# First pair's neighbour scores spread by TensorE and masked from PSUM; the output weights' column sums moved behind the first attention

## The chip, the cores and the metric

The kernel runs on one core of a Trainium2 chip. A core has five engines with an instruction queue each: TensorE (PE; its weight loads are listed apart as PEld), VectorE (DVE), ScalarE (ACT), GpSimd (POOL) and SyncE (SP), which issues most of the DMAs; ScalarE issues some. Data lie in SBUF or, for TensorE's results, in PSUM (eight banks of 128 partitions by 512 f32). The metric is the device time of one execution in microseconds (us); lower is better.

## What is computed

128 graphs of 128 nodes with 512 features each go through a graph attention layer (8 heads of 64 units) and a hypergraph convolution, each with a residual and a layer norm. Cut to what matters here:

```python
# layer 0, per graph; A is the 0/1 adjacency
feats = X @ W[h]                                   # 8 heads of 64
e_self, e_neigh = feats . a_self, feats . a_neigh  # two scores per node and head
dense = leaky_relu(e_self[:, None] + e_neigh[None, :], 0.2) + NEG_BIG * (1 - A)
out = relu(softmax(dense) @ feats + b)
x = layernorm(x + out)
# layer 1; R = D^-1 H B^-1 H^T from the adjacency
h = layer_norm(relu(R @ (x @ W1^T) + b1), gamma, beta)
x = layernorm(x + (R @ (h @ W2^T) + b2) + x)
```

All of it is f32.

## The kernel before

**Tiling.** The graphs go in 64 pairs. A pair passes through five overlapping stages, T = 38.6 planned us apart: loads and masks; features and scores; softmax and attention; the hidden product; output and store. In the steady state TensorE runs without gaps, using Strassen's seven products for 2x2 blocks of the weights (`chain`, copied by line 329), which need sums of weight blocks: four of `w0` (`prepare_first_sums`, line 211), four of `w1` (`prepare_hidden`, line 234), and four of `w2` (`prepare_output_block_sums`).

**Order.** Every step is a small function with a due time. `steps` holds those of all pairs, `first` gives other times for single steps of the first pairs, `todo` holds what is done once (weights and their preparation). All are sorted by time and emitted in that order, which is then the order of each engine's queue, and of each DMA queue. An engine takes its instructions strictly in that order, so one that waits holds up all behind it. Only the order counts, not the planned times.

**The first pair (p = 0).** Its features are 32 plain products (line 510), copied into `ft` with the two scores as the first two columns of each head (line 520). To spread a neighbour's score over all partitions, `spread_rows` transposes the score columns into `rows` (line 529), writes them to DRAM by four DMAs (line 537, two on SP, two on ScalarE's queue), and `neighbours` reads them back to all 128 partitions, 512 KB for each graph, as `nb` (line 557). GpSimd then adds the mask `neg` in four quarters (`masked`, line 576; a quarter is one graph g and one half of the heads, q). ScalarE adds a node's own score and applies the leaky relu (`leaky`, line 592); for the last quarter of the first pair VectorE does so (lines 585 and 588). VectorE takes the negated maximum (`largest`, line 598), ScalarE the exponential (line 606). `e_transpose_first` turns the first pair's exponentials by TensorE (line 638), with the copies to `eT` shared by VectorE and ScalarE (line 639). `attend` multiplies by the features (line 662), `attended` divides (lines 676 and 677), GpSimd adds the bias (686), VectorE the residual and the moments (693 to 707), GpSimd takes the power for the inverse deviation (709), ScalarE normalises (725 to 734) into `y`. `propagate` multiplies `y` by R (line 757, `pz`), ScalarE evicts it to `zT` (769), GpSimd makes its block sums `zS` (780), and the hidden products follow (792).

**Second pair.** Its rows go out in one DMA (539), its scores come back in two (557), into the same buffer `nb`, of which there is one: the reading has to wait until the first pair's exponentials are transposed. It has its masks, leaky relu, maxima and exponentials while the first pair is in the hidden products; ScalarE's copies of `phX`, which TensorE waits for before it adds the next product to that bank, stand in the same ScalarE queue.

**Nodes and edges.** For R: `nodes` (345 to 354) and `edges` (406 to 413) count on VectorE, `scale_edges` (420) scales, `propagator` multiplies (429), `r_evict` (437) scales again with `dnb`, which has gone through DRAM. For the first two pairs `edges` reads a transposition in PSUM.

**The output weights.** gamma and the mean are folded into `w2`: `prepare_output` forms two column sums (gamma/DH and beta) with 16 small products, 32 records (261, `pv`), `prepare_output_sums` copies them (269), `prepare_output_spread` spreads them over the partitions as `gw` and `bw` (273), `prepare_output_bias` copies `bw` (278), and `prepare_output_blocks` scales and shifts the four blocks of `w2` on VectorE, four instructions each (285).

Of the kernel before, what the change touches and what calls it, by code (L numbers as in the profile page):

```python
# [8 lines left out]
F32 = mybir.dt.float32  # L9
AF = mybir.ActivationFunctionType  # L10
ALU = mybir.AluOpType
# [3 lines left out]
SLOPE = 0.2  # L15
# [5 lines left out]
def kernel(  # L21
# [45 lines left out]
    nc = tc.nc  # L67
    G, N, F = x.shape
    P = 128
    DH = w1t.shape[1]  # L70
    H = 8
# [17 lines left out]
    def bank(name):  # L89
        return psum.tile([P, HALF], F32, tag="bank", name=name)  # L90
# [433 lines left out]
    @step(1, 25.0)  # L524
    def spread_rows(p, s):


        rows = work.tile([P, B], F32, tag="rows", name=f"rows_{p}")
        nc.vector.transpose(
            rows.rearrange("p (c x) -> p c x", c=2),  # L530
            s["ft"][:, :, :, :2].rearrange("p g h c -> p c (g h)"),
        )
        shape = [B, NB, B] if p == 0 else [NB, B, B]
        rd = s["rd"] = dram.tile(shape, F32, tag="rd", name=f"rd_{p}")
        if p == 0:
            for b in range(NB):
                (nc.sync, nc.scalar)[b % 2].dma_start(rd[:, b, :], rows[b * B:(b + 1) * B])
        else:
            nc.sync.dma_start(rd.rearrange("b c j -> (b c) j"), rows)
# [6 lines left out]
    @step(1, 27.0)  # L546
    def neighbours(p, s):
        s["nb"] = work.tile([P, 2, H * N], F32, tag="nb", name=f"nb_{p}")
        for g in range(2):
            dst, src, hs = s["nb"][:, g, :], s["rd"], slice((2 + g) * H, (3 + g) * H)  # L550
            if p == 0:
                src = src[hs].rearrange("h b j -> (h b j)")
            else:
                dst = dst.rearrange("p (b x) -> p b x", b=NB)
                src = src[:, hs, :].rearrange("b h j -> b (h j)")
            queue = nc.scalar if p == 0 and g == 1 else nc.sync
            queue.dma_start(dst, src.partition_broadcast(P))
# [10 lines left out]
    def scores(p, s, g, hs):  # L568
        return blocked(p, s["nb"][:, g, :])[:, :, hs, :]
# [3 lines left out]
    def masked(p, s, g, q):  # L573
        t = scores(p, s, g, slice(q * HH, (q + 1) * HH))
        neg = s["neg"][:, g].rearrange("p (b j) -> p b j", b=NB)
        nc.gpsimd.tensor_tensor(  # L576
            t, t, neg[:, :, None, :].to_broadcast([P, NB, HH, B]), op=ALU.add
        )

    def leaky(p, s, g, q):  # L580
        if (p, g, q) == (0, 1, 1):

            hs = slice(HH, H)
            t = s["nb"][:, g, HH * N:].rearrange("p (h j) -> p h j", h=HH)
            nc.vector.tensor_tensor(
                t, t, s["ft"][:, g, hs, 0:1].to_broadcast([P, HH, N]), op=ALU.add
            )
            nc.vector.scalar_tensor_tensor(t, t, SLOPE, t, op0=ALU.mult, op1=ALU.max)
            return
        for h in range(q * HH, (q + 1) * HH):  # L590
            t = scores(p, s, g, h)
            nc.scalar.activation(t, t, AF.Prelu, bias=s["ft"][:, g, h, 0:1], alpha=SLOPE)  # L592
# [432 lines left out]
    for t, fn, *args in (  # L1025
# [28 lines left out]
        (98.1, prepare_output_bias, ()), (98.2, prepare_output_blocks, (slice(0, 1),)),  # L1054
        (99.75, prepare_output_blocks, (slice(1, 2),)),
# [17 lines left out]
        ("leaky", 0, 1, 1): 77.65,  # L1073
# [12 lines left out]
    for p, time, fn, *args in (  # L1086
# [84 lines left out]
```

## Time and profile before

The median of four runs is 2528.41 us (2528.16 to 2528.68). The profiled execution took 2528.16 us; its span, from the first to the last instruction, is 2526.4 us.

| | PE | DVE | ACT | POOL |
|---|---|---|---|---|
| busy, us of the span | 2498.9 | 1919.8 | 1539.6 | 1792.4 |
| share | 99% | 76% | 61% | 71% |

From the timeline of the first pair and of the start of the second, us from the span's start:

| | start | end |
|---|---|---|
| first pair's features (510), last copy (520) | 10.63 | 20.69 |
| scores broadcast from DRAM (557), issue to landing | 23.55 | 28.4 |
| first pair's masks on GpSimd (576) | 28.38 | 33.33 |
| column sums `pv` (261) | 29.46 | 36.53 |
| first pair's exponentials (606) | 33.31 | 38.08 |
| first pair's attention `pav` (662), with the last transposition between | 38.98 | 43.20 |
| first `pz` (757) | 50.70 | 54.40 |
| second pair's first maximum (598) | 56.28 | 56.97 |
| pace of a pair in the steady state (`pyX` at 239.31, 277.97, 316.64) | 38.67 | |

How to read it: an instruction group is given by its line in the source, engine, operation, output and inputs. A busy engine is not by itself the bound; the wait that ends last in a stage is. A f32 product of 128x128 by 128 shows as two records of TensorE, a transposition as one.

### The profile page before, as it was taken

How to read it: one execution, taken by the hardware profiler on the slowest of the kernel's cores; microseconds unless marked ns; L12 is line 12 of the kernel's file. 1: busy time of each engine (PE TensorE's matmuls, PEld its weight loads, DVE VectorE, ACT ScalarE, POOL GpSimd, SP SyncE). 2: the span in 40 equal slices, each digit the busy share in tenths (PEclk: the TensorE clock that was granted, in tenths of full speed). 3: DMA queues.
4: the chain of work that ended last, by engine and by line, in shares of the span. 5: the costliest groups of instructions: out<-in, count | busy, mean ns of one | idle time of the engine just before them, and what ended most of it. 6: DMA issues, size and time to landing. Idle time of an engine off the chain costs nothing.

```text
span 2526.4 us, 48492 instructions
## 1 busy us (share of the span) xinstructions
PE 2498.9 (99%) x16349; PEld 2269.8 (90%) x16349; DVE 1919.8 (76%) x4332; ACT 1539.6 (61%) x4481; POOL 1792.4 (71%) x2058
## 2 busy tenths in 40 slices
PE   7999999999999999999999999999999999999998
PEld 5899999999999999999999999999899999999997
DVE  7877777777777777777777777777777777777765
ACT  4565665755756656657557566566575665665753
POOL 5867777776777677767766776777677767777774
PEclk9999999999999999999999999999999999999999
DMA  6545445444444454454454444544544444445431
GB/s 184 135 135 142 137 132 152 132 129 147 132 135 142 137 143 137 128 151 134 125 152 133 136 139 139 144 136 125 152 131 130 145 137 140 137 131 151 134 110 51
DMA packets 420840, 343.76 MB, mean 136 GB/s; under 512 B 141272, under 2 KB 370160, under 8 KB 420592
## 3 DMA queue, kind: packets, MB, share of 16 engines
q1 hardware_dynamic: 417120, 336.19, 45.0%
q10 hardware_dynamic: 3472, 4.47, 0.6%
q8 instruction: 131, 2.15, 0.3%
q14 instruction: 117, 0.96, 0.1%
HBM read 238.83 MB, written 101.71 MB: 135 GB/s over the span
## 4 chain that ended last, share of the span: by engine, by line
PE 97%; DVE 1%; DMA 1%; issue 0%; POOL 0%; ACT 0%; SPq 0%; POOLq 0%; DVEq 0%; ACTq 0%
PE phX L792 18%; PE pyX L473 17%; PE phW L792 9%; PE pfX L473 9%; PE pav L662 9%; PE pyW L473 8%; PE pz L757 5%; PE phY L792 4%; PE pq L919 4%; PE pfW L473 4%; PE pyY L473 4%; PE pfY L473 2%; PE pd L429 1%; PE pf L510 1%; PE pm L887 1%
## 5 line engine op out<-in xcount | busy, mean ns | idle before, releaser
L329 ACT COPY py<-pyX 128x257 f32<-128x257 f32 x189 | 70.8, 375 | 539.3 <-PE pyX L473 523.3
L792 PEld LDWEIGHTS phX<-zS,w_sb 128*128 128x128 f32 x3072 | 363.1, 192 | 33.0 <-issue 31.6
L792 PE MATMUL phX<-zS,w_sb 128*128 128x128 f32 x3072 | 374.3, 275 | 2.4 <-POOL xS L455 1.3
L845 POOL TENSOR_TENSOR sq<-sq 128x512 f32<-128x512 f32 (+2 forms) x384 | 344.4, 897 | 20.4 <-ACT sq L833 0.3
L576 POOL TENSOR_TENSOR nb<-nb,neg 128x512 f32<-128x512 f32 x256 | 318.5, 1278 | 7.3 <-DMA nb<-rd 7.3
L592 ACT ACTIVATE nb<-nb,ft 128x128 f32<-128x128 f32 x1020 | 317.3, 389 | 7.1 <-POOL nb L576 7.1
L598 DVE TENSOR_REDUCE nm<-nb 128x4 f32<-128x512 f32 x256 | 174.7, 683 | 188.4 <-ACT nb L592 126.6
L606 ACT ACTIVATE nb<-nb,nm 128x128 f32<-128x128 f32 x1024 | 313.5, 392 | 0.4 <-DVE nm L598 0.4
L709 POOL TENSOR_TENSOR rso<-veo,mhalf 128x2 f32<-128x2 f32 x63 | 44.2, 702 | 372.9 <-DVE veo L707 372.9
L662 PEld LDWEIGHTS pav<-ft,eT 128*128 128x128 f32 x2048 | 248.4, 192 | 8.6 <-DVE eT L639 0.8
L662 PE MATMUL pav<-ft,eT 128*128 128x65 f32 x2048 | 242.8, 272 | 0.0
L473 PE MATMUL pyX<-w_sb,hS 128*128 128x257 f32 x1008 | 242.5, 382 | 0.0
L822 ACT ACTIVATE h<-h,vecs 128x128 f32<-128x128 f32 x768 | 239.7, 392 | 2.2 <-DVE h L807 2.2
L473 PE MATMUL pyX<-w_sb,h 128*128 128x257 f32 x1008 | 239.5, 379 | 0.5 <-ACT py L329 0.5
L473 PE MATMUL pyW<-w_sb,hS 128*128 128x256 f32 x1008 | 238.6, 378 | 0.3 <-DVE y L876 0.3
L473 PEld LDWEIGHTS pyW<-w_sb,hS 128*128 128x128 f32 x1008 | 190.6, 189 | 27.9 <-DVE y L876 0.7
L686 POOL TENSOR_TENSOR y<-y,b_bc 128x512 f32<-128x512 f32 x128 | 162.9, 1273 | 68.0 <-DVE y L677 68.0
L473 PEld LDWEIGHTS pyX<-w_sb,h 128*128 128x128 f32 x1008 | 186.3, 190 | 25.6 <-ACT py L329 0.9
L473 PEld LDWEIGHTS pyX<-w_sb,hS 128*128 128x128 f32 x1008 | 186.1, 190 | 24.4
L909 DVE SCALAR_TENSOR_TENSOR y<-y,rsh,bw_bc 128x512 f32<-128x512 f32 x126 | 148.6, 1217 | 53.6 <-POOL rsh L905 53.5
L627 DVE STREAM_TRANSPOSE eT<-eb 128x512 f32<-128x512 f32 x252 | 163.1, 684 | 1.7 <-DMA eb<-ed 1.6
L833 ACT ACTIVATE sq<-h 128x512 f32<-128x512 f32 x256 | 160.5, 628 | 2.1
(167 smaller groups left out, 5647.0 us busy)
## 6 DMA issues: line engine op xcount, KB each, us to landing
nb<-rd SPq DMA_DIRECT2D x127, 512.0 KB, 6.7
ed<-nb SPq DMA_DIRECT2D x126, 512.0 KB, 2.6
eb<-ed SPq DMA_DIRECT2D x504, 128.0 KB, 2.9
x<-in_x_dram SPq DMA_DIRECT2D x64, 512.0 KB, 9.5
out_dram<-o SPq DMA_DIRECT2D x63, 512.0 KB, 2.8
xb<-in_x_dram SPq DMA_DIRECT2D x248, 128.0 KB, 3.0
a<-in_adj_dram SPq DMA_DIRECT2D x64, 128.0 KB, 8.3
w<-in_adj_dram SPq DMA_DIRECT2D x128, 64.0 KB, 7.0
```

The source lines that it names most:

```text
L473: nc.tensor.matmul(to[:, :n], lhs[:, k, :], rhs[:, k, :n], start=bool(start) and k == 0, stop=(k == nk - 1), skip_group_check=True,)
L576: nc.gpsimd.tensor_tensor(t, t, neg[:, :, None, :].to_broadcast([P, NB, HH, B]), op=ALU.add)
L592: nc.scalar.activation(t, t, AF.Prelu, bias=s["ft"][:, g, h, 0:1], alpha=SLOPE)
L598: nc.vector.tensor_reduce(s["nm"][:, g, hs], scores(p, s, g, hs).rearrange("p b h j -> p h b j"), AX.XY, ALU.max, negate=True,)
L606: nc.scalar.activation(t, t, AF.Exp, bias=s["nm"][:, g, h:h + 1])
L627: nc.vector.transpose(s["eT"][:, g, hs, :].rearrange("p h (b i) -> p h b i", b=NB), s["eb", g][:, :, hs, :].rearrange("p b h j -> p h b j"),)
L662: nc.tensor.matmul(t[:, h * (U + 1):(h + 1) * (U + 1)], s["eT"][:, g, q * HH + h, :], s["ft"][:, g, q * HH + h, 2:], start=True, stop=True,)
L686: nc.gpsimd.tensor_tensor(s["y"][:, g, :], s["y"][:, g, :], b0_bc, op=ALU.add)
L792: nc.tensor.matmul(to[:, m * N:(m + 1) * N], w[:, k, m * P:(m + 1) * P], rhs[:, k, :], start=bool(start) and m == 0 and k == 0, stop=(k == ...
L822: nc.scalar.activation(dst[:, k, :], src[:, k, :], AF.Relu, bias=b1_sb[:, c:c + 1])
L833: nc.scalar.activation(s["sq"][:, g, q * KH // 2:(q + 1) * KH // 2, :], hid(s, g, q), AF.Square, scale=DH ** -0.5,)
L845: nc.gpsimd.tensor_tensor(t[:, :n, :], t[:, :n, :], t[:, n:2 * n, :], op=ALU.add)
```

## The change

The first pair's scores no longer go through DRAM. `neighbours_first` multiplies, for each head, the score column of `ft`, repeated 128 times as the stationary operand, by the identity: 16 products into four PSUM banks. `masked` of the first pair adds `neg` on VectorE, from PSUM into `nb`. All four quarters' leaky relu is ScalarE's.

The column sums of the output weights, their spreading and the scaling of the first two blocks come later: the sums behind the first attention, the spreads behind the first `pz`, the blocks ahead of the third one. The four `w0` sums, the first pair's edges and the second pair's nodes, rows and feature copies are placed later too. All four blocks of `w1` are loaded from SP, in the order 3, 1, 0, 2, and GpSimd's three sums of them are made in the order 0, 1, 2, the third behind the power of the first layer norm.

```diff
-    @step(1, 25.0)
+    @step(1, 25.0, since=1)
     def spread_rows(p, s):
...
-        shape = [B, NB, B] if p == 0 else [NB, B, B]
-        rd = s["rd"] = dram.tile(shape, F32, tag="rd", name=f"rd_{p}")
-        if p == 0:
-            for b in range(NB):
-                (nc.sync, nc.scalar)[b % 2].dma_start(rd[:, b, :], rows[b * B:(b + 1) * B])
-        else:
-            nc.sync.dma_start(rd.rearrange("b c j -> (b c) j"), rows)
+        rd = s["rd"] = dram.tile([NB, B, B], F32, tag="rd", name=f"rd_{p}")
+        nc.sync.dma_start(rd.rearrange("b c j -> (b c) j"), rows)
...
-    @step(1, 27.0)
+    @step(1, 27.0, since=1)
     def neighbours(p, s):
...
+    def neighbours_first(p, s, g, q):
+        t = s["pnb", g, q] = bank(f"pnb_{g}{q}")
+        for h in range(HH):
+            nc.tensor.matmul(
+                t[:, h * N:(h + 1) * N],
+                s["ft"][:, g, q * HH + h, 1:2].to_broadcast([P, N]), ident,
+                start=True, stop=True,
+            )
...
     def masked(p, s, g, q):
+        if p == 0:
+            if (g, q) == (0, 0):
+                s["nb"] = work.tile([P, 2, H * N], F32, tag="nb", name=f"nb_{p}")
+            nc.vector.tensor_tensor(
+                s["nb"][:, g, q * HALF:(q + 1) * HALF].rearrange("p (h j) -> p h j", h=HH),
+                s["pnb", g, q].rearrange("p (h j) -> p h j", h=HH),
+                s["neg"][:, g][:, None, :].to_broadcast([P, HH, N]), op=ALU.add,
+            )
+            return
...
     def leaky(p, s, g, q):
-        if (p, g, q) == (0, 1, 1):
...
-            return
...
-        (11.1, prepare_first, (0,)), (12.0, prepare_first, (1,)), (15.45, prepare_first_sums, ()),
+        (11.1, prepare_first, (0,)), (12.0, prepare_first, (1,)), (108.1, prepare_first_sums, ()),
...
-        (14.05, load_weights, (nc.scalar, w1_blocks[:2], w1t, F // 2, HALF)),
-        (15.46, load_weights, (nc.sync, w1_blocks[:1:-1], w1t, F // 2, HALF)),
+        (15.46, load_weights, (nc.sync, [w1_blocks[i] for i in (3, 1, 0, 2)], w1t, F // 2, HALF)),
...
-        (79.0, prepare_hidden, (nc.gpsimd, 2)), (79.1, prepare_hidden, (nc.gpsimd, 0)),
-        (79.2, prepare_hidden, (nc.gpsimd, 1)), (110.6, prepare_hidden, (nc.vector, 3)),
-        (15.5, prepare_output_vectors, ()), (16.0, prepare_output, ()),
-        (78.3, prepare_rows, ()), (78.79, prepare_output_sums, ()),
-        (78.92, prepare_output_spread, (0, "gw")), (98.0, prepare_output_spread, (1, "bw")),
-        (98.1, prepare_output_bias, ()), (98.2, prepare_output_blocks, (slice(0, 1),)),
-        (99.75, prepare_output_blocks, (slice(1, 2),)),
+        (79.0, prepare_hidden, (nc.gpsimd, 0)), (79.1, prepare_hidden, (nc.gpsimd, 1)),
+        (108.05, prepare_hidden, (nc.gpsimd, 2)), (110.6, prepare_hidden, (nc.vector, 3)),
+        (15.5, prepare_output_vectors, ()), (97.9, prepare_output, ()),
+        (78.3, prepare_rows, ()), (108.2, prepare_output_sums, ()),
+        (116.75, prepare_output_spread, (0, "gw")), (116.76, prepare_output_spread, (1, "bw")),
+        (121.85, prepare_output_bias, ()), (116.8, prepare_output_blocks, (slice(0, 1),)),
+        (116.82, prepare_output_blocks, (slice(1, 2),)),
         (117.8, prepare_output_blocks, (slice(2, 3),)),
...
-        ("spread_rows", 0): 13.5, ("neighbours", 0): 14.0,
+        ("mask", 0): 12.05, ("mask", 2): 118.5, ("masked", 0): 13.3,
...
-        ("edges", 0): 14.46, ("edges", 2): 119.2,
-        ("x_transpose", 2, 0): 120.5, ("x_transpose", 2, 1): 121.1, ("scale_edges", 0): 14.47, ("propagator", 0): 14.55,
+        ("edges", 0): 78.67, ("edges", 2): 119.2,
+        ("x_transpose", 2, 0): 120.5, ("x_transpose", 2, 1): 121.1, ("scale_edges", 0): 78.68, ("propagator", 0): 78.75,
...
-        ("spread_rows", 1): 15.72, ("nodes", 1): 15.55, ("write_nodes", 1): 15.85,
-        ("edges", 1): 110.4, ("scale_edges", 1): 110.5, ("neighbours", 1): 80.1,
+        ("spread_rows", 1): 78.72, ("nodes", 1): 78.7, ("write_nodes", 1): 78.705,
+        ("edges", 1): 110.4, ("scale_edges", 1): 110.5, ("neighbours", 1): 78.74,
...
-        (0, 13.0, plain_features_out), (1, 13.1, x_transpose_out, 0), (1, 13.8, x_transpose_out, 1),
+        (0, 13.0, plain_features_out), (0, 13.2, neighbours_first, 0, 0),
+        (0, 13.21, neighbours_first, 0, 1), (0, 13.22, neighbours_first, 1, 0),
+        (0, 13.23, neighbours_first, 1, 1), (1, 13.1, x_transpose_out, 0), (1, 13.8, x_transpose_out, 1),
         (1, 14.5, plain_features, 0), (1, 14.6, plain_features, 1),
-        (1, 15.6, plain_features_out), (1, 97.9, adj_transpose_first),
+        (1, 78.71, plain_features_out), (1, 97.9, adj_transpose_first),
```

As the queues stand after the change: on VectorE, between the variance of the first layer norm and the second pair's first maximum, come the four `w0` sums, the copies of the column sums, the second pair's edges and their scaling, the fourth `w1` sum, and twelve instructions of `prepare_output_blocks`. On GpSimd, the third `w1` sum, three masks of the second pair, the third pair's `neg`, and the four `zS`. On TensorE, after the first `pz`, the two spreads, then the second pair's propagator and the hidden products.

More of the change, by code (lines that the diff above doesn't have):

```diff
@@ L549, in neighbours @@
         for g in range(2):
[L550 to L557, printed above, removed]
+            nc.sync.dma_start(
+                s["nb"][:, g, :].rearrange("p (b x) -> p b x", b=NB),
+                s["rd"][:, (2 + g) * H:(3 + g) * H, :].rearrange("b h j -> b (h j)")
+                .partition_broadcast(P),
+            )
[7 more added lines that the diff above has]
+            )
     @step(1, 28.0)
@@ L573, in masked @@
     def masked(p, s, g, q):
+        if p == 0:
[5 more added lines that the diff above has]
+                s["neg"][:, g][:, None, :].to_broadcast([P, HH, N]), op=ALU.add,
+            )
+            return
         t = scores(p, s, g, slice(q * HH, (q + 1) * HH))
@@ L580, in leaky @@
     def leaky(p, s, g, q):
-        if (p, g, q) == (0, 1, 1):
[L583 to L588, printed above, removed]
-            return
         for h in range(q * HH, (q + 1) * HH):
@@ L1064 @@
     first = {
-        ("spread_rows", 0): 13.5, ("neighbours", 0): 14.0,
+        ("mask", 0): 12.05, ("mask", 2): 118.5, ("masked", 0): 13.3,
         ("nodes", 0): 12.9, ("write_nodes", 0): 12.92, ("spread_nodes", 0): 15.9,
-        ("edges", 0): 14.46, ("edges", 2): 119.2,
-        ("x_transpose", 2, 0): 120.5, ("x_transpose", 2, 1): 121.1, ("scale_edges", 0): 14.47, ("propagator", 0): 14.55,
+        ("edges", 0): 78.67, ("edges", 2): 119.2,
+        ("x_transpose", 2, 0): 120.5, ("x_transpose", 2, 1): 121.1, ("scale_edges", 0): 78.68, ("propagator", 0): 78.75,
         ("r_evict", 0): 99.76,
-        ("spread_rows", 1): 15.72, ("nodes", 1): 15.55, ("write_nodes", 1): 15.85,
-        ("edges", 1): 110.4, ("scale_edges", 1): 110.5, ("neighbours", 1): 80.1,
+        ("spread_rows", 1): 78.72, ("nodes", 1): 78.7, ("write_nodes", 1): 78.705,
+        ("edges", 1): 110.4, ("scale_edges", 1): 110.5, ("neighbours", 1): 78.74,
         ("propagator", 1): 117.76, ("spread_nodes", 1): 80.3, ("r_evict", 1): 121.8,
-        ("leaky", 0, 1, 1): 77.65,
+        ("leaky", 0, 1, 1): 77.65, ("largest", 0, 1, 1): 77.66,
         ("attend", 0, 0, 0): 78.95, ("attend", 0, 0, 1): 78.96, ("attend", 0): 97.85,
```

## The prediction

> **What bounds the kernel now.** I read the page's busy shares first, then what TensorE (PE) waited for, then the windows and the timeline of the stretch where it waited longest. Columns of a timeline line: start and length in us, engine, source line, operation, tiles, and in brackets the idle time before it.
>
> ```profile
> PE 2498.9 (99%) x16349; PEld 2269.8 (90%) x16349; DVE 1919.8 (76%) x4332; ACT 1539.6 (61%) x4481; POOL 1792.4 (71%) x2058
> ```
>
> TensorE is busy for 99% of the span, so a change to the first pairs is worth only what it does to TensorE's early gaps. The waits up to 130 us (total, times, longest) name them:
>
> ```profile
> PE px L382 <- DMA x<-in_x_dram: 8.8, 1, 8.8
> PE pz L757 <- ACT y L734: 6.2, 1, 6.2
> PE phX L792 <- ACT zT L769: 1.7, 1, 1.7
> PE phX L792 <- POOL xS L455: 1.3, 1, 1.3
> PE phX L792 <- ACT ph L329: 1.1, 1, 1.1
> ```
>
> The large one that the change can reach is the 6.2 us ahead of the first propagation `pz`. It has a second price, which the windows show (length, then busy us of PE, PEld, DVE, ACT, POOL, then granted TensorE clock, DMA share, GB/s): the clock is at half while the sixteen records of `pz` run.
>
> ```profile
> 44.40:50.60 6.20, 0.08 (x1) 0.00 (x0) 5.70 (x15) 1.93 (x6) 3.91 (x4) 0.74 0.79 166
> 50.60:54.20 3.60, 3.50 (x16) 3.51 (x17) 3.60 (x4) 1.33 (x3) 2.52 (x3) 0.50 0.00 0
> ```
>
> VectorE (DVE) is busy for 5.70 of those 6.20 us and for all of the next 3.60. Its timeline there, with GpSimd (POOL):
>
> ```profile
> 48.45 0.17 DVE L707 TENSOR_SCALAR vea<-mva 128x2 f32<-128x2 f32 x1
> 48.71 0.72 POOL L709 TENSOR_TENSOR rsa<-vea,mhalf 128x2 f32<-128x2 f32 x1 [1.77 <-DVE vea L707]
> 49.39 3.73 POOL L576 TENSOR_TENSOR nb<-nb,neg 128x512 f32<-128x512 f32 x3
> 49.47 2.50 DVE L420 TENSOR_SCALAR hB<-hT,deg 128x128 f32<-128x128 f32 x2
> 51.89 2.31 DVE L234 TENSOR_TENSOR w_sb<-w_sb 128x1024 f32<-128x1024 f32 x1
> 54.12 1.64 DVE L285 SCALAR_TENSOR_TENSOR w_sb<-w_sb,vecs,gw 128x256 f32<-128x256 f32 x4
> 56.28 0.69 DVE L598 TENSOR_REDUCE nm<-nb 128x4 f32<-128x512 f32 x1 [0.51 <-POOL zS L780]
> ```
>
> Two things are to be seen. The two L420 scalings take 2.50 us beside GpSimd's masks; two of the same at 21.86, with GpSimd idle, took 0.48. Each ends as one mask ends: VectorE waits for GpSimd's instruction, and then one of the other goes. L234 likewise ends 1.08 us after the third mask. So VectorE's operations on two SBUF inputs, and its tensor_scalars from SBUF, alternate with GpSimd's; L285 and L598 don't. And the second pair's first maximum (L598, done at 56.97) stands behind all this: behind it are ScalarE's exponentials, and in ScalarE's queue behind those the evictions of `phX` that two of the listed waits are for.
>
> **The change, step by step.** All times are from the span's start.
>
> *Scores by TensorE.* The write of `rows` (landed 23.3), the two 512 KB broadcasts (to 28.4) and GpSimd's four masks (28.38 to 33.3) go. In their place stand 16 products of 128x128, 32 records. The nearest row is `pz` at 93.70, 16 records in 1.95, 0.112 each: 3.6 us. Bounds: 1.8 at the pace of the 16 transposes L638, 7.2 at half clock; I take 3.6, since it is the same shape at the clock granted here. They start behind `vecs_T` at 20.6 and push the second pair's feature products to 24.2 to 31.3. The four additions from PSUM have no row; nearest are L807 (PSUM and SBUF in, 0.65 to 0.69) below and GpSimd's 1.27 above: 0.69, behind each quarter of the products, so done at 25.1. ScalarE's 16 leaky activations (12 took 3.73) run 22.5 to 27.3, VectorE's fourth maximum ends at 28.0, and the exponentials (4.77 for 16) at 31.95 where they ended at 38.08.
>
> *First collision.* The `w1` loads no longer stand behind the broadcasts. All four are on SP's queue from 19.0 instead of 23.9; at the 300 to 370 GB/s of the windows a block lands each 1.4 to 1.8 us behind the last of `w2` (22.1), the third at about 27.3. So GpSimd's two sums L234 (2.38 and 2.36 there) move from 35.6 to about 26.0 to 30.8, onto VectorE's moved edges of the first pair, whose tensor_scalar would start at 28.5: it waits to 30.8, and the edges end at 31.4 instead of 29.4. Price 2.0; bounds 0 and 2.4, one whole L234. In VectorE's queue behind them stand the second pair's nodes (1.34, as at 25.01), its feature copies (four at a pace of 0.34, a transposition), and then the copy of `eT` that attention waits for: 35.05. The four attention products took 38.98 to 43.20, 4.22 with the last transposition between; now 35.15 to 39.4. `y` is complete 0.7 later, 40.1 against 44.83, and the variance (L707) 3.8 after that, as now: 43.9 against 48.62, **4.7 earlier**.
>
> *Column sums.* The 32 records L261 (7.01) move from ahead of the transpositions to behind attention: 39.2 to 46.2. They cover the wait for `pz`, which starts at 46.4 against 50.70, and hold the clock: 1.8 instead of 3.70. On TensorE they cost nothing while y needs 2.08 from the variance to `pz` (48.62 to 50.70); uncovered, 7.0. The two spreads L273 (1.12 each at most) follow `pz`, where TensorE waits for the eviction of `pz` anyhow.
>
> *What VectorE must do before the second pair's maximum.* Between L707 and the end of L598 it took 8.35 us (48.62 to 56.97). Added there: the four `w0` sums L211 (0.70 each; at 22.26 with GpSimd idle, in a wait for the broadcasts), the copies of the column sums (0.84), and eight more L285 (two groups of 1.64). GpSimd has its third L234 there too, then the three masks. Alternating as above, from 43.9 as zero: sums one and two to 1.4, L234 to 3.6 (it runs 2.2 once free), sum three 4.2, mask 5.3, sum four 5.9, copies 6.7, edges' PSUM reads 7.1, their small tensor_scalar behind the third mask 8.3, scalings among GpSimd's `neg` and `zS` 9.4, VectorE's L234 11.2, twelve L285 at 0.392 to 15.8, L598 16.5. That is 60.4 against 56.97: **3.4 later**. Bounds: 11.7 if nothing collides (55.6, or 53.5 if the first collision too is absent: 3.4 earlier), 17.5 if the power L709 also blocks (4.5 later). I take 16.5, since the alternation shows at 49.47, 98.50 and 66.95.
>
> *Behind it* everything to the fourth product's start (66.41) keeps its distance of 9.44: exponentials, the eviction copies, the next maxima. The moved copy of `bw` (0.59) sits in ScalarE's queue ahead of the third quarter's exponentials, but the fourth waited 0.40 for its maximum anyway: 0.1. DMAs: on SP the four `w1` blocks now stand ahead of `dnb` (31.20 now; then about 23, free of the broadcasts, landing near 30 for its use at 38) and of `b2` and `xb`, with no one waiting. The second pair's rows, node weights and scores move behind these; the scores are issued at 37.7, once the first pair's transpositions free `nb` (41.56 now), land within about 7.5, by 45.2, and are masked from 47.5.
>
> *The clock again.* TensorE goes idle from 61.0, when the first four of the hidden products are done, to 66.3, when the copy behind the exponentials lets the fifth start: 5.3 us. One row speaks for each side: 6.22 idle cost the clock, 1.68 at 97.33 did not. If it goes, the fifth product takes 3.7 instead of 1.95 and perhaps the next also; TensorE has 1.7 to 2.2 of slack up to 97.33 (waits of 0.27, 0.25, 1.68). Bounds 0 and 3; I take 1.0.
>
> The Trainium skill, "TensorE: Matmul & The Clock Gate", section "HAM oscillation — how this bites in real kernels", holds that no gap may exceed about 3.4 us. By it the clock surely goes in the new gap, and the term is nearer 2, the sum 5.4. The row at 44.40 agrees but has no gap between 1.7 and 6.2.
>
> The Trainium skill, "SBUF — State Buffer", section "SBUF: two separate sides", calls the port that the two engines share an exclusive lock for the whole instruction. By it L709 would block as well, giving the 17.5. Here L412 took its 0.17 in the midst of L709, so the measurement decides.
>
> **Sum.** 3.4 + 1.0 = 4.4 on the profiled execution (span 2526.4, its time 2528.16, 1.76 around it), whose remaining 38.67 us a pair are not touched. The median of the runs is 2528.41, 0.25 above: 2532.8.
>
> **The rivals.**
> 1. *The clock drop stays.* The gap of 5.3 us halves the clock through the fifth to seventh products, the features come late for VectorE's `ft` sums (at 79.68, ahead of `rows` in its queue), and the chain at 97.33 moves with them: 2.1 to 4.6 on top of 3.4, +5.5 to +8. It decides once TensorE's delay exceeds its 2.2 of slack. For it: half clock lasted 6.8 us the last time. Against it: most TensorE work there waits for ScalarE. 2533.9 to 2536.4.
> 2. *The engines hardly collide.* The `w1` blocks land early enough for GpSimd to finish by 28.5, and it lets VectorE's sums pass in one go: 3.4 earlier up to 1.5 later, 2525.0 to 2529.9. For it: VectorE has its sums queued at the very moment that L709 ends. Against it: each pair of operands above alternated.
> 3. *VectorE isn't the bound.* Then all of the earlier `pz` and its clock stay: 4.3 + 1.9, 6.2 earlier, 2522.2. Against it: twelve L285 stand ahead of the maximum in the queue, which by itself allows no more than 3.4.
>
> **How the numbers follow.** A measurement of this kernel can tell about 0.2% (5.06 us) from no change. The forecast (+2 to +6.5) has 0.55, of which 0.33 below 5.06 and 0.22 above; rival 1 0.22, all slower; rival 2 0.13, all within; rival 3 0.10, faster. So faster 0.10, same 0.46, slower 0.44. The range takes in rival 2 and nearly all of rival 1: 2525.0 to 2537.0; the forecast alone gives 2530.4 to 2534.9.
>
> **What would show it.** Right: `pz` at about 46.4 in 1.8 us at clock 1.00; L234 on GpSimd beside a stretched L412 or L420 near 29; the four L211 spread over some 6 us with L234 and masks between; the first maximum of the second pair ending near 60; a TensorE gap near 61 to 66. Wrong: that maximum before 56, the sums in 2.8 us, or `pz` not earlier than 49.

## The result and the profile after

| | before | after |
|---|---|---|
| median of the runs, us | 2528.43 (61 runs, 2526.94 to 2530.10) | 2530.97 (41 runs, 2529.55 to 2533.67) |
| profiled execution: time, span, us | 2528.16, 2526.4 | 2531.53, 2529.7 |
| variance of the first pair's `y` (L707/708) ends | 48.62 | 43.75 |
| `pz` starts, its duration | 50.70, 3.70 | 46.68, 1.95 |
| second pair's first maximum (L598/599) ends | 56.97 | 59.10 |
| first hidden product of the second pair (`phX`) starts | 97.33 | 99.97 |
| from there to the end of the span | 2429.1 | 2429.7 |

The ratio of the two is 1.0011, with a 95% interval of 1.0007 to 1.0016: 2.5 us more, which is clear of the noise but within the 0.2% (5.06 us) that the prediction had put down as no change. 2532.8 had been forecast. The lines for `phX`, before and after:

```profile
97.33 2.05 PE L792 MATMUL phX<-zT,w_sb 128*128 128x128 f32 x16 [1.68 <-ACT zT L769]
```

```profile
99.97 2.05 PE L793 MATMUL phX<-zT,w_sb 128*128 128x128 f32 x16 [1.16 <-ACT zT L770]
```

The waits of TensorE up to 130 us after the change (total, times, longest):

```profile
PE px L382 <- DMA x<-in_x_dram: 9.1, 1, 9.1
PE phX L793 <- ACT ph L329: 3.0, 1, 3.0
PE gw L273 <- DVE sums L269: 1.8, 1, 1.8
PE phX L793 <- ACT zT L770: 1.2, 1, 1.2
PE pav L663 <- DVE eT L640: 1.0, 1, 1.0
```

The 6.2 us ahead of `pz` are gone, and in its place stand smaller waits further on. The windows show what happened to the clock (columns as in the prediction: length, then busy us of PE, PEld, DVE, ACT, POOL, granted clock, DMA share, GB/s):

```profile
46.40:48.60 2.20, 2.20 (x19) 2.03 (x18) 2.20 (x2) 0.46 (x1) 2.20 (x2) 1.00 0.04 5
52.00:56.00 4.00, 3.72 (x17) 3.42 (x17) 3.96 (x10) 3.41 (x10) 2.69 (x5) 0.57 0.02 4
62.00:65.00 3.00, 0.00 (x0) 0.03 (x1) 2.93 (x7) 3.00 (x10) 0.00 (x0) 1.00 0.43 175
66.00:72.00 6.00, 5.28 (x26) 5.01 (x25) 4.42 (x6) 4.66 (x15) 5.91 (x5) 0.51 0.57 179
```

`pz` now runs at full clock, but half clock returns at 52 to 56, and again from 66 to 72, behind a wait of 3.0 us. TensorE's lines there, `pz` and the product behind that wait:

```profile
46.68 1.95 PE L758 MATMUL pz<-R,y 128*128 128x128 f32 x16
65.00 2.76 PE L793 MATMUL phX<-zS,w_sb 128*128 128x128 f32 x16 [3.02 <-ACT ph L329]
```

VectorE is busy throughout. The main lines of its timeline from the variance to the maximum, with GpSimd's lines beside them:

```profile
43.58 0.17 DVE L708 TENSOR_SCALAR vea<-mva 128x2 f32<-128x2 f32 x1
44.39 0.71 DVE L211 TENSOR_TENSOR w_sb<-w_sb 128x528 f32<-128x528 f32 x1
45.02 2.87 DVE L211 TENSOR_TENSOR w_sb<-w_sb,w 128x528 f32<-128x528 f32 x1
47.81 1.77 DVE L211 TENSOR_TENSOR w_sb<-w_sb 128x528 f32<-128x528 f32 x1
49.51 0.73 DVE L269 COPY sums<-pv 2x256 f32<-2x256 f32 x2
50.69 1.26 DVE L412 TENSOR_SCALAR deg<-deg 128x2 f32<-128x2 f32 x1
52.18 0.48 DVE L420 TENSOR_SCALAR hB<-hT,deg 128x128 f32<-128x128 f32 x2
52.58 1.22 DVE L234 TENSOR_TENSOR w_sb<-w_sb 128x1024 f32<-128x1024 f32 x1
58.42 0.68 DVE L599 TENSOR_REDUCE nm<-nb 128x4 f32<-128x512 f32 x1
```

```profile
44.91 2.42 POOL L234 TENSOR_TENSOR w_sb<-w_sb,w 128x1024 f32<-128x1024 f32 x1
47.29 4.64 POOL L586 TENSOR_TENSOR nb<-nb,neg 128x512 f32<-128x512 f32 x3
```

The third sum takes 2.87 instead of 0.70: it ends 0.5 behind GpSimd's L234 (47.33). The fourth likewise ends 0.6 behind the first mask (49.02), and the tiny L412 (0.17 alone) takes 1.26, up to the end of the third mask (51.93). Those are the collisions that the forecast counted on; L420 and VectorE's L234, counted with them, ran free. Earlier, ahead of attention, another small operation had met GpSimd:

```profile
26.06 1.92 DVE L247 TENSOR_SCALAR gbs<-vecs 128x8 f32<-128x8 f32 x1
```

```profile
25.58 2.37 POOL L234 TENSOR_TENSOR w_sb<-w,w_sb 128x1024 f32<-128x1024 f32 x1 [3.11 <-DMA w<-in_w1t_dram]
```

### The profile page after: what moved, and what is told of

Read it like the earlier page. It is cut to its first block, busy times and chain, and to the rows that moved or that the text cites. A ratio compares the mean times of both kernels' runs of the same rounds, so it can differ in the third digit from the quotient of the medians.

```text
span 2529.7 us, 48548 instructions
## 1 busy us (share of the span) xinstructions
PE 2505.2 (99%) x16381; PEld 2277.1 (90%) x16381; DVE 1926.2 (76%) x4333; ACT 1540.7 (61%) x4485; POOL 1788.2 (71%) x2054
## 3 DMA queue, kind: packets, MB, share of 16 engines
q1 hardware_dynamic: 417424, 336.70, 45.2%
## 4 chain that ended last, share of the span: by engine, by line
PE 96%; DVE 1%; DMA 1%; ACT 1%; issue 1%; POOL 0%; SPq 0%; POOLq 0%; DVEq 0%; ACTq 0%
PE phX L793 18%; PE pyX L473 17%; PE pfX L473 9%; PE phW L793 9%; PE pav L663 9%; PE pyW L473 8%; PE phY L793 4%; PE pfW L473 4%; PE pz L758 4%; PE pq L920 4%; PE pyY L473 4%; PE pfY L473 2%; PE pd L429 1%; PE pm L888 1%; PE py L963 0%
## 5 line engine op out<-in xcount | busy, mean ns | idle before, releaser
L710 POOL TENSOR_TENSOR rso<-veo,mhalf 128x2 f32<-128x2 f32 x63 | 44.2, 701 | 373.1 <-DVE veo L708 373.1
```

## The experiments

All times are medians, and each ratio, with its 95% interval, is to the kernel before measured beside it on the same chip (2528.2 to 2528.7). Positions are from one profiled execution of each run. In the diffs, lines of the changed kernel's plan stand with "-".

**Single parts of VectorE's list moved behind the maximum.** First the four `w0` sums:

```diff
-        (108.1, prepare_first_sums, ()),
+        (123.2, prepare_first_sums, ()),
```

> The changed kernel with the four w0 sums (L211) moved in VectorE's queue from behind the first layer norm's variance to behind the second pair's fourth maximum; nothing else. Theory A (VectorE's queue between that variance and the second pair's first maximum sets the time): in the changed kernel the sums stood from 43.66 to 49.58. Without them the maximum, which ended at 59.10, ends at 56 to 57.8, since the edges' scaling then collides with GpSimd's masks instead; 1.3 to 3 us off the changed kernel. Rival B (the half clock from 66 to 72 us is what the change costs): no more than 1 us, unless the clock holds. Rival C (the copies of zT wait for the two spreads, because sel lies in zT's buffer; they ran at 52.4 where pz was done at 48.6): the spreads come 2.7 us earlier, so up to 2.7 us too, but with the maximum still directly behind L285.

Measured: 2535.72, ratio 1.0030 (1.0018 to 1.0042), 4.7 above the changed kernel. A miss. The maximum ended at 58.90, hardly earlier, since the variance came at 45.23 (TensorE had waited 1.55 for `eT`, and attention ran at half clock), VectorE now waited for the column sums, and its L412 and L420 met the masks instead. And in their new place the sums met GpSimd again:

```profile
69.33 2.67 DVE L211 TENSOR_TENSOR w_sb<-w_sb 128x528 f32<-128x528 f32 x1
71.92 2.56 DVE L420 TENSOR_SCALAR hB<-hT,deg 128x128 f32<-128x128 f32 x2
74.40 0.68 DVE L808 TENSOR_TENSOR h<-ph,phW 128x512 f32<-128x512 f32 x1
```

```profile
75.13 3.78 PE L793 MATMUL phW<-zT,w_sb 128*128 128x128 f32 x16 [4.82 <-DVE h L808]
```

L808, which frees TensorE's bank, stood behind them: TensorE lost 4.82 us (in the bracket) and its clock (0.55 from 74.5 to 82).

Then the eight instructions L285 of the first two blocks of `w2`, then both edits, and, against a rival, `sel` alone in a buffer of its own. This rival came from the trace after: `sel`, which the spreads read, lies in the buffer of `zT`, so ScalarE's copies of `pz` (done at 48.6) began only when the spreads ended:

```profile
52.38 1.07 ACT L770 COPY zT<-pz 128x512 f32<-128x512 f32 x2 [5.51 <-PE bw L273]
```

```diff
# blocks late (with the edit above: both late)
-        (116.8, prepare_output_blocks, (slice(0, 1),)),
-        (116.82, prepare_output_blocks, (slice(1, 2),)),
+        (123.3, prepare_output_blocks, (slice(0, 1),)),
+        (123.4, prepare_output_blocks, (slice(1, 2),)),
# sel on its own (alone)
-        made["sel"] = work.tile([2, 2, P], F32, tag="zT", name="sel")
+        made["sel"] = const.tile([2, 2, P], F32, name="sel")
```

> The changed kernel with the scaling of the first two w2 blocks (eight L285, 53.72 to 56.9) moved behind the second pair's fourth maximum. Theory A: the first maximum ends 3.2 us earlier, at 55.9, and the time falls by about 3 us, to 0.5 us below the kernel before. Rival B: 1 us or less. Rival C: nothing, since the spreads and zT stay where they are.

> Both moves. Theory A: first maximum at about 54.6, 4 to 5 us off the changed kernel, some 2 us below the kernel before; TensorE's gap near 62 shrinks under 2 us and the clock stays at full. Rival B: the gain is larger than the earlier maximum, by the clock. Rival C: as the first run, no more than 2.7.

> The changed kernel with sel in a buffer of its own, so that zT needn't wait for the spreads. Theory A: zT's copies go from 52.4 to about 47.7 and 48.5, but the maximum stays behind VectorE's L285 and no time is gained; zS now runs among VectorE's scalings and its w1 sum and delays these, 0 to 1.3 us slower. Rival C: 2 to 3 us faster.

Measured: blocks late 2530.50, ratio 1.0009 (1.0000 to 1.0018); both late 2532.13, 1.0017 (1.0008 to 1.0026); `sel` on its own 2531.41, 1.0014 (1.0005 to 1.0023). With the blocks late the maximum ended at 55.53, 3.6 earlier, as expected, but the second pair's `phX` came only 1.1 earlier (98.86), so the time missed what was expected. Of the 3.0 that were lost on the way, 1.1 were lost ahead of the moved L285, where VectorE's third maximum waited 0.95 for ScalarE. The rest came behind them: the eight L285 (3.3 us) stand ahead of the next L808 and `eT`, for which TensorE then waited (0.26 and 0.81). Both late missed for the reason of the sums (TensorE waited 5.9 for L808). The buffer of `sel` costs nothing in the sum: with its own buffer `zT` is copied at 47.88 instead of 52.38, but GpSimd's block sums, which are then earlier too, meet VectorE's list, and the maximum ended 0.6 later (59.69), as expected.

**Each half alone.** The scores by TensorE, with all else of the change but the column sums as before, and the column sums behind attention, with all else as before:

```diff
# scores alone: from the changed kernel
-        (97.9, prepare_output, ()),
+        (16.0, prepare_output, ()),
...
-        (108.2, prepare_output_sums, ()),
-        (116.75, prepare_output_spread, (0, "gw")), (116.76, prepare_output_spread, (1, "bw")),
-        (121.85, prepare_output_bias, ()), (116.8, prepare_output_blocks, (slice(0, 1),)),
-        (116.82, prepare_output_blocks, (slice(1, 2),)),
+        (78.79, prepare_output_sums, ()),
+        (78.92, prepare_output_spread, (0, "gw")), (98.0, prepare_output_spread, (1, "bw")),
+        (98.1, prepare_output_bias, ()), (98.2, prepare_output_blocks, (slice(0, 1),)),
+        (99.75, prepare_output_blocks, (slice(1, 2),)),
# columns alone: the reverse, from the kernel before
```

> The scores by TensorE as in the changed kernel (with its order of loads, and the four w0 sums behind the variance), but the column sums where they were before: their 32 products ahead of the transpositions, spreads, copies and eight L285 behind attention. Theory A (VectorE's list ahead of the second pair's first maximum is the bound): the products of the column sums hold TensorE to about 39.4, attention starts near 40 as before, the variance ends near 48, the wait ahead of pz with its half clock is back, and the list behind the variance still has the four sums beside GpSimd's L234 and masks (about 12.5 us without the eight L285 and the copies), so the maximum ends near 60.5: 2531 to 2533. Rival (the earlier scores and loads are worth something by themselves): the maximum ends by 57, 2527 or less.

> The kernel before with the column sums alone moved behind attention's products, as in the changed kernel; scores, masks, loads and the four w0 sums as before. Theory A: attention as before (from 38.98), the 32 products fill the wait for pz, which starts near 50.5 at full clock in 1.9 instead of 3.7, but the copies and eight more L285 (4.1 us together) stand ahead of the second pair's first maximum, which ends near 60.5 to 61: 2530 to 2532. Rival (the clock kept at pz and the covered wait decide): gain of 1.8 or more, 2526.5 or less.

Measured: 2535.21, ratio 1.0028 (1.0017 to 1.0040), and 2535.22, ratio 1.0027 (1.0017 to 1.0037): each half alone costs 7.0, both together 2.5. VectorE's list from variance to maximum took 12.48 and 12.50, as expected (12.5 each). What was missed is the variance, 50.63 and 51.23 instead of some 48.5. With the scores alone their 32 records stand ahead of everything on TensorE: the column sums start at 31.16 instead of 29.46, and attention at 41.17 instead of 38.98. With the column sums alone TensorE has nothing to do while the scores go through DRAM, VectorE's L588 meets GpSimd's L234 (2.73 instead of 0.69), and attention runs at half clock:

```profile
28.80:33.80 5.00, 0.01 (x1) 0.01 (x1) 2.32 (x5) 4.09 (x14) 4.87 (x5) 0.85 0.95 325
33.80:46.70 12.90, 11.41 (x48) 9.83 (x49) 7.76 (x13) 5.47 (x17) 8.86 (x7) 0.50 0.56 122
```

The column sums' 32 records had been holding the clock there. So each half alone costs more than both: one takes TensorE's wait away at 30, the other at 45.

**The sums in waits where GpSimd is idle.** VectorE waits at 18.0, 19.9 and 21.7; before the change the sums had run free in such a place.

```diff
-    def prepare_first_sums():
-        second_sums(nc.vector, [w0_sb[:, i] for i in range(7)], w0_12)
+    def prepare_first_sums(some):
+        second_sums(nc.vector, [w0_sb[:, i] for i in range(7)], w0_12, some)
...
-        (108.1, prepare_first_sums, ()),
+        (12.93, prepare_first_sums, (slice(0, 2),)), (13.25, prepare_first_sums, (slice(2, 4),)),
...
-        (15.5, prepare_output_vectors, ()),
+        (13.31, prepare_output_vectors, ()),
...
-        ("masked", 0): 13.3,
+        ("masked", 0, 0, 0): 13.3, ("masked", 0, 0, 1): 13.3,
+        ("masked", 0, 1, 0): 13.32, ("masked", 0, 1, 1): 13.32,
```

> The changed kernel with the four w0 sums in VectorE's waits at 18 and near 21.8, where GpSimd is idle, and gbs between the masks, ahead of GpSimd's first L234. Theory A (both collisions cost what they show, 1.8 and 3.1 beyond the sums' own 2.8): the sums take 0.7 each, the masks start at most 0.4 later, the first pair's maxima begin near 26.5 instead of 27.96, the sums are gone from behind the variance, and the second pair's first maximum ends near 55.5 to 57 instead of 59.1, which is then set by the column sums' products (done at 46.5) and the twelve L285; the clock stays through 66 to 72. Some 3 us faster than the changed kernel: 2527 to 2528.5. Rival (the loss lies elsewhere, in what TensorE waits for behind 66): at most 1 faster, 2530 or more.

> The edits of the two kernels together: w0 sums and gbs early, and the eight L285 of the first two blocks behind the second pair's maxima as in the experiment with the blocks late. Theory A: the maximum ends near 52 to 53, six earlier than in the changed kernel, and since 5.9 us of sums are gone from VectorE's busy stretch altogether, the work put off no longer comes late for the next use: 2525 to 2527, ahead of the kernel before. Rival (what TensorE waits for behind 70 takes the place): no better than the earlier of its two parts, 2528 or more.

Measured: 2530.60, ratio 1.0010 (1.0001 to 1.0018), and with the blocks late too 2531.07, 1.0008 (0.9999 to 1.0017). Both missed. The sums did take 0.67 to 0.90 each, and the first pair's maxima began at 24.85. But the edges met GpSimd's L234 (L412 at 28.61 took 2.13, the very collision that the prediction had named), `eT` came no earlier, and TensorE, done sooner with the features, waited for it: 1.85 us idle, and then half clock for some 10 us in which it was busy without a break. The windows of the run with the sums early:

```profile
33.40:35.25 1.85, 0.00 (x0) 0.00 (x0) 1.82 (x6) 0.18 (x1) 0.00 (x0) 1.00 0.07 13
36.50:47.00 10.50, 10.50 (x40) 6.77 (x40) 5.87 (x16) 0.81 (x3) 3.69 (x4) 0.51 0.52 143
```

The variance came 2.4 later than in the changed kernel, and the maximum at 60.11. The clock fell once more there, from 57 to 60.5, and this time behind no wait: from 36 to 64 TensorE was idle for 0.03 us in all. The two spreads of the column sums, whose operands have two rows, stand at 53.45 to 55.4. With `eT` first (the next run) the same spreads ran and the clock held, so what made it fall is open.

```profile
54.00:56.00 2.00, 2.00 (x8) 0.87 (x6) 2.00 (x5) 0.54 (x2) 0.00 (x0) 1.00 0.03 8
58.00:60.00 2.00, 2.00 (x11) 2.00 (x11) 2.00 (x5) 1.45 (x4) 2.00 (x4) 0.50 0.00 0
```
With the blocks late as well, L285 and L420 again stood ahead of L808 (71.28), and TensorE waited 2.3 for it.

**`eT` before the second pair's features, then the other waits filled.**

```diff
# eT first (with the sums early)
-        ("spread_rows", 1): 78.72, ("neighbours", 1): 78.74,
+        ("spread_rows", 1): 78.88, ("neighbours", 1): 78.89,
...
-        (1, 78.71, plain_features_out),
+        (1, 78.87, plain_features_out),
# waits filled (with eT first, and sel on its own)
-        (110.6, prepare_hidden, (nc.vector, 3)),
+        (108.04, prepare_hidden, (nc.vector, 3)),
...
-        ("edges", 1): 110.4, ("scale_edges", 1): 110.5,
+        ("edges", 1): 99.75, ("scale_edges", 1): 99.755,
...
-        (1, 97.9, adj_transpose_first),
+        (1, 79.31, adj_transpose_first),
```

> As the run with the sums early, and VectorE copies the first eT before the second pair's feature copies (which have 1.4 us of work ahead of it). In the run with the sums early TensorE waited 1.85 us for eT and ran at half clock from 36.5 to 47, so that attention took 6.6 instead of 4.1 and the products of the column sums 9.4 instead of 7.0. Theory A (that wait cost the clock, and the second pair's first maximum sets the time at a constant distance of 40.3 us to the second pair's phX): eT at 33 to 33.5, no wait of TensorE above 0.7, full clock up to pz, variance at 42 to 43, pz near 45, the maximum near 56 to 57, phX of the second pair near 96.5 to 97.3: 2527 to 2528.5, 2 to 4 less than the changed kernel, and no spread of runs up to 2533. Rival (the clock falls whatever is done there, for instance since the products with two columns keep TensorE too little busy): half clock again before 47, maximum at 59 or later, 2530 or more.

> As the run with eT first, and VectorE's other work ahead of the maximum goes into its waits too: the second pair's edges (with TensorE's transposition behind the last of the first pair's) into its wait for attention, its L234 directly behind the variance into its wait for the column sums; sel in a buffer of its own. Theory A: behind the column sums (near 45) only their spreads and twelve L285 are left, the maximum ends near 53 to 54, and with the constant distance of 40.3 the second pair's phX starts near 93.5 to 95: 2524 to 2526, ahead of the kernel before by 2 to 4. Rival (past some 56 another engine, ScalarE or GpSimd, holds the second pair, so an earlier maximum is not worth its length): 2527 to 2528.5, as the run with eT first.

Measured: 2527.43, ratio 0.9997 (0.9988 to 1.0005), and 2528.89, ratio 1.0000 (0.9991 to 1.0009). With `eT` first the same two windows are:

```profile
33.40:35.25 1.85, 1.85 (x18) 1.70 (x16) 1.62 (x4) 0.68 (x2) 0.00 (x0) 1.00 0.08 13
36.50:47.00 10.50, 10.50 (x64) 6.04 (x63) 7.44 (x24) 2.68 (x6) 6.96 (x5) 1.00 0.58 154
```

64 records instead of 40 in the same 10.5 us; the variance at 42.87, the maximum at 56.39, and a median 3.2 us below the run with the sums early, as expected, for one copy's place in a queue. The clock did fall later in this execution, behind a wait of 4.55 that ended at 62.30. The run with the other waits filled missed in its median (2524 to 2526 expected): the maximum ended at 54.68 and the profiled execution was 2526.01, but only 4 of 11 executions were like it (2526.0 to 2527.3, clock 0.999 to 1.0); 7 took 2528.8 to 2529.7 at 0.997 to 0.998.

**Is that the clock?** TensorE still had waits of 1.92 and 2.69 in the profiled execution. The next run shortens both (the first pair's hidden product number 5, the fourth to be issued, is computed twice into the same place as a filler); the last one puts that filler alone into the changed kernel.

```diff
# waits and warm (with the waits filled)
-        (108.04, prepare_hidden, (nc.vector, 3)),
+        (108.3, prepare_hidden, (nc.vector, 3)),
# both
             at(lag, t, product, i, since=since, until=until)
+            if kind == "ph" and i == 5:
+                at(lag, t + 0.01, again, i, until=1)
...
+        def again(p, s, i):
+            multiply(s, i, s[kind, "W"], 1)
```

> As the run with the waits filled, with two edits against its waits of TensorE, which in that run's single executions go with two groups of times (2526 to 2527.3 at a granted clock of 0.999 to 1.0, and 2528.8 to 2529.7 at 0.997 to 0.998): VectorE's L234 stands behind the copies of the column sums instead of directly behind the variance, so that GpSimd's power is not held up and the wait of 1.92 ahead of pz falls to 1.0; and the first pair's fifth hidden product is issued a second time into the same place, 1.9 us of TensorE work in its wait of 2.69. Theory A (the slower group is the one whose clock falls in these waits): one group only, 2524.5 to 2526.5, ahead of the kernel before by 2 to 4. Rival (the groups have another cause, a DMA's arrival for instance): two groups again, median 2527 to 2529.

> The changed kernel, in which only the first pair's fifth hidden product is issued twice: it fills the wait of TensorE from 62 to 65, behind which its clock was at half from 66 to 72. Theory A: the clock stays full there, the second pair's phX starts near 99.4 (the maximum's end at 59.1 plus the constant 40.3) instead of 99.97, the slower group of its runs (2532 to 2533.7) vanishes: 2530 to 2530.5, some 0.5 to 1 below the changed kernel's median; the clock's term of the prediction is then of that size. Rival (half clock there hides behind other waits): 2531 and the same spread.

Measured: 2526.53, ratio 0.9992 (0.9983 to 1.0001), all 11 executions from 2525.83 to 2527.21 at full clock; and 2531.66, ratio 1.0012 (1.0003 to 1.0021). The first has one group only: the upper one is gone, and only the two waits were touched (by VectorE's L234 moved and by the filler). So the upper group came from those waits. That the clock fell in them is likely, by the clocks of the two groups, but no execution of the upper group was profiled. The lines of that run (they are five lines further down in its code):

```profile
53.88 0.68 DVE L604 TENSOR_REDUCE nm<-nb 128x4 f32<-128x512 f32 x1
```

```profile
60.48 2.02 PE L798 MATMUL phX<-zS,w_sb 128*128 128x128 f32 x16 [0.91 <-ACT ph L332]
94.90 2.05 PE L798 MATMUL phX<-zT,w_sb 128*128 128x128 f32 x16 [1.69 <-ACT zT L775]
```

Its gain, 2.1, is at the lower end of the 2 to 4 that were expected: the maximum was no earlier than with the waits filled (54.56), since it waits for the spreads of the column sums and twelve L285. The 21 executions of the kernel before beside it took 2527.56 to 2529.40, all above its own 11; by the interval, which reaches 1.0001, the gain is just short of shown.

The filler alone missed: its time is the one that the rival gave, and the spread stayed (2530.54 to 2533.02). It did its work in its place (full clock from 60 on, and 40.37 from the maximum to `phX` instead of 40.87), but in that execution `eT` came late for TensorE, as in the run with the sums early, and the clock fell there:

```profile
34.43 2.16 PE L668 MATMUL pav<-ft,eT 128*128 128x65 f32 x16 [1.55 <-DVE eT L645]
```

```profile
38.00:43.00 5.00, 5.00 (x19) 3.29 (x19) 2.69 (x7) 0.06 (x1) 2.10 (x2) 0.51 0.63 167
```

Six profiled executions have the same code up to the variance, and they show what that place is worth:

| execution | wait for `eT` | clock, 36 to 44 | variance |
|---|---|---|---|
| changed kernel | 0.95 | 1.00 | 43.75 |
| `sel` on its own | 1.13 | 1.00 | 43.86 |
| blocks late | 1.20 | 1.00 | 43.31 |
| sums late | 1.55 | 0.57 | 45.23 |
| both late | 1.55 | 0.57 | 45.19 |
| filler alone | 1.55 | 0.57 | 45.02 |

So the same start takes 1.2 to 1.9 us longer when TensorE waits 1.55 for `eT`, and the single runs above have to be read with that in mind. The changed kernel has at least two places where the clock may fall, one of which (62 to 65) the prediction had seen. That these make its own runs spread by 4 us is likely, but was not shown by a run that closes both and nothing else.

## Why the prediction was right, and where not

The way to the result is one chain, and the runs give each link (us from the span's start):

| run | variance | list of VectorE | maximum ends | to second pair's `phX` | `phX` |
|---|---|---|---|---|---|
| before | 48.62 | 8.35 | 56.97 | 40.36 | 97.33 |
| after | 43.75 | 15.35 | 59.10 | 40.87 | 99.97 |
| sums late | 45.23 | 13.67 | 58.90 | 46.49 | 105.39 |
| blocks late | 43.31 | 12.22 | 55.53 | 43.33 | 98.86 |
| both late | 45.19 | 10.96 | 56.15 | 47.52 | 103.67 |
| `sel` on its own | 43.86 | 15.83 | 59.69 | 40.63 | 100.32 |
| scores alone | 50.63 | 12.48 | 63.11 | 40.32 | 103.43 |
| columns alone | 51.23 | 12.50 | 63.73 | 40.36 | 104.09 |
| sums early | 46.15 | 13.96 | 60.11 | 40.30 | 100.41 |
| early and blocks late | 45.69 | 12.26 | 57.95 | 43.34 | 101.29 |
| eT first | 42.87 | 13.52 | 56.39 | 41.17 | 97.56 |
| waits filled | 43.19 | 11.49 | 54.68 | 40.29 | 94.97 |
| waits and warm | 43.97 | 10.59 | 54.56 | 40.34 | 94.90 |
| filler alone | 45.02 | 15.34 | 60.36 | 40.37 | 100.73 |

From `phX` to the end of the span it is 2428.9 to 2429.9 in every run. The distance is 40.3 to 40.4 wherever no work is put behind the maximum and the clock holds from some 64 us on; half clock ahead of that cost nothing (scores alone, from 60.5 to 63.6). That carries the prediction's main claim: VectorE's list in front of that maximum sets the time. The claim rests on this table more than on the median, since the stated range, 2525.0 to 2537.0, would have taken in two of the rivals too.

1. *Scores by TensorE.* Right: 32 records in 3.84 (3.6 predicted), the additions from PSUM 0.69 each, as taken from L807.
2. *First collision.* The price was right (1.8 for 2.0), the place in this execution was not: the small `gbs` (L247, 1.92 instead of 0.16) met GpSimd's first L234 at 26.06, and the edges behind it ran free. In four of the other five executions with the same start (those with the sums, the blocks or both late, and with `sel` on its own) `gbs` ran free and the edges met GpSimd, as predicted (L412 1.59 to 2.19); in the one with the filler neither did. The variance came at 43.75 for 43.9. That is partly luck: another collision happened to cost the same, and in three of the six executions the variance came at 45.0 to 45.2, by a clock loss in attention that the prediction had not considered.
3. *Cover of `pz`.* Right: 46.68 for 46.4, 1.95 for 1.8, clock 1.00.
4. *VectorE's list.* The mechanism held, the size was too large by 1.15: 15.35 for 16.5. Up to the end of L412 each step is within some 0.2 of the list (the four sums 5.8 for 5.9). The power did not hold up the sums beside it (0.70 and 0.71), as the prediction had taken it, but was itself held up (L710 1.10 instead of 0.72). Then L420 and L234 ran without GpSimd, 1.2 less. About 0.5 of that is the buffer of `sel`, which the prediction had overlooked: it kept GpSimd's `zS` waiting for `zT` until the spreads were done. With `sel` on its own the list took 15.83. The maximum came 2.1 later, not 3.4.
5. *Everything behind keeps its distance.* Right: the product that was to keep its 9.44 started 9.39 behind the maximum (68.49), and the table shows the distance up to `phX`. Behind that the prediction had taken nothing; 0.7 came there, and no run shows from what (the runs differ by 1.0 in that part).
6. *The clock.* The wait was 3.0 (62.0 to 65.0), not 5.3, and yet the clock went, to 0.51 over 66 to 72. Its price was 0.5 (40.87 against 40.36), half of the 1.0 taken, and 0.8 in the run with `eT` first (half clock from about 63 to 70). The slack that the prediction named, 1.7 to 2.2, took up the rest: TensorE was 2.1 late at the next pair's first feature product (74.25, which is 15.15 behind the maximum, where it was 13.09 before). Not foreseen was half clock at 52 to 56, behind a wait of 1.76 for the copies of the column sums. It cost nothing: the run with the filler alone had it from 53 to 60, and its distance was 40.37.

Together: 2.1 + 0.5 to `phX`, and 0.7 behind it in this execution, 3.3 on the profiled span, against 4.4. The 2.5 in the medians is nearer still to no change because of which executions were profiled: that of the kernel before lies 0.3 below its median, that of the changed kernel 0.6 above.

*The rivals.* That the engines hardly collide is out: 5.8 us for sums of 2.8. That VectorE is not the bound is out by the table. That the clock drop stays is half right: it occurs, but is worth 0.5 to 0.8, not 2.1 or more, since TensorE's delay stayed inside its slack. Where the gain went is then clear: 4.9 us of an earlier variance were spent on 7.0 us more in VectorE's list, and by the rows these are 4.0 for the column sums' copies and eight L285, 2.8 for the `w0` sums and 3.0 for their waiting, while the later collisions changed hands: 1.1 more for L412, 3.1 less for L420 and L234, which had met the masks before the change, and 0.8 less in waits and gaps.

The Trainium skill, "TensorE: Matmul & The Clock Gate", section "HAM oscillation — how this bites in real kernels", allows gaps of up to about 3.4 us. The runs differ: a gap of 3.0 lost the clock in the changed kernel and one of 1.85 in the run with the sums early, while one of 2.69 kept it in the profiled execution with the waits filled.

## What to carry to other kernels

When one wait of a pipeline's start is removed, follow the queue of the busiest other engine up to the next instruction that somebody waits for: work that had been hidden in the old wait now stands in front of it. Put such work where its engine waits and the engine that it collides with is idle, rather than merely later. Here moving it later gave nothing that is clear of the spread (2530.5 at best, against 2531.0), while moving it into earlier waits, with `eT` copied first and TensorE's waits shortened, turned +2.5 into -2.1. And in the first 100 us one copy's place in a queue can cost 3 us, when the TensorE that waits for it loses its clock.

## What the runs showed of the hardware

- The clock fell behind gaps of TensorE of 3.0 (changed kernel at 62), 1.85 (sums early) and 1.55 (sums late, both late, the filler alone). It did not behind 0.95, 1.13 and 1.20 ahead of attention, nor, in one execution, behind 2.69. It also fell with no gap ahead (sums early at 57). The same kernel does either in different executions: with the waits filled, 4 executions at a clock of 0.999 to 1.0 and 7 at 0.997 to 0.998, some 2.5 us apart.
- Once it had fallen it stayed at half for some 3.4 us (52.4 to 55.8) or more than 6 (66 to 72) in the changed kernel and, with TensorE busy in every record, for some 10 (36.6 to 46.9) with the sums early.
- VectorE's smallest operations, a tensor_scalar on 128x2 or 128x8, can wait for a whole instruction of GpSimd: 1.26 and 2.13 for L412, 1.92 for L247, against 0.16 to 0.17 alone. In the kernel before, L412 took its 0.17 in the midst of GpSimd's power (49.07, L709 from 48.71 to 49.43). It goes the other way too: that power (L710) took 1.62 beside VectorE's L234 with the waits filled, where it takes 0.71 with the sums early.
